# A gated cross-attention block on one core: the step of the feed-forward integers taken from the row's magnitude alone, and the last two turns in a new order

## Chip, cores and metric

The kernel runs on one core of a Trainium2 chip. Its time is the device time of one execution in microseconds (us). The engines are PE (TensorE, matrix products), PEld (its weight loads), DVE (VectorE), ACT (ScalarE), POOL (GpSimd) and SP (SyncE, which here issues DMAs). Each engine works through its own list of instructions in order; semaphores hold an instruction until what it needs is there.

## What is computed

`x` has 4 x 512 rows of 512 numbers, `ctx` 4 x 1024. An attention part with 16 heads comes first, over all 2048 rows against all 4096 context rows, with quantised queries, keys, values and weights of attention. Then comes the feed-forward part, the only one that matters here:

```python
def rms_norm(x):
    return x * jax.lax.rsqrt(jnp.mean(x * x, axis=-1, keepdims=True) + EPS)

def act_quant(x):
    scale = 127.0 / jnp.clip(jnp.max(jnp.abs(x), axis=-1, keepdims=True), 1e-05)
    q = jnp.clip(jnp.round(x * scale), -128.0, 127.0) / scale
    return x + jax.lax.stop_gradient(q - x)

def bitlinear158(x, w, b):
    xq = act_quant(rms_norm(x))
    wq = weight_quant(w)          # -1, 0 or 1, times one step for the matrix
    return jnp.einsum('bsd,od->bso', xq, wq) + b

h = jax.nn.silu(bitlinear158(x, w1, b1))      # 2048 wide
h = jax.nn.gelu(h, approximate=False)
h = layer_norm(h, ln_g, ln_b)
return bitlinear158(h, w2, b2)

x = x + jnp.tanh(g_xattn[0]) * xattn(_layernorm(x), ctx, ...)
x = x + jnp.tanh(g_ffn[0]) * ffn(_layernorm(x), ...)
```

The integers of a row are the row, divided by its largest magnitude and multiplied by 127, rounded. The factor of `rms_norm` is one number for a row, so it multiplies the row and its largest magnitude alike and falls out of the integers; it is still needed for the step by which the product of the integers is multiplied in the end.

## The kernel before

The 2048 rows are 16 tiles of 128. The attention part (about the first 1480 us) runs head by head, with an order of work that is planned by units. The feed-forward part takes the tiles in eight groups of two (`GT = 2`, `NGT = 8`). For group g, with tiles 2g and 2g + 1, these steps follow each other:

- `load_x`, `load_o`, `bias_x` (POOL adds a bias to `X`), `steps_x`, `wide_step` (ACT, L974), `turned_steps` (PE, four transposes, L987), `scale_o` (DVE, L996), `project` (PE, L1003), `residual_x` (DVE, L1009 to L1014: `X` and its mean and variance). This ends the attention part.
- `factors_x` (POOL, L892 to L900): from the variance the factor of the layer norm and of `rms_norm`, with powers. `integers_x` (DVE, L1021 to L1042): subtract the mean and multiply by the factor, largest magnitude, scale, integers. It also makes `dq1`, the step of the first product, and its inverse in three bf16 parts (L1035, L1037; on POOL for g > 0), with which the bias rides along in the product. `turned_x` (PE, L1049), `turned_x_out` (ACT, L1056).
- `hidden`: `first_product` in two halves a tile (PE, L1073, L1077; ten matmuls a half, into two PSUM buffers `ph` in turn), `silu` (ACT, L1083, scaled by `dq1`). `gelu` (ACT, L1094, with the row sum; POOL makes minus the mean of it, `nm`, at L1098). `variance` (ACT, squares of `h + nm`, L1102 by way of `squares`). `factors_h` (POOL, L907, L908): the factor `rh` of the layer norm.
- `normal` (DVE): `centred` (L1117), `normal_rows` (L1124), `magnitudes` (L1130, largest magnitude `ah`). `norm_squares` (ACT, L1102: the sum of squares `ss`). `factors_q` (POOL, L916 to L928, nine instructions): the factor of `rms_norm`, the scale `sc` of the integers and the step `dq2`.
- `integers_h` (ACT, L1181, then a transposing DMA issued by SP, L1184), `result` (PE, L1194, L1197), `bias_y` (POOL, L979), `residual_y` (DVE, L1203, then the store by SP, L1206).

`turn(s)` writes out the order for all engines of one turn by hand. It works on five groups at once: projection of group gx = s + 2, integers_x of gi = s + 1, first product, silu, gelu and variance of s, normal and norm_squares of gn = s - 1, integers_h and result of gy = s - 2. `turn` runs for s = 1 to 6; `last_turns` writes out what is left: all of group 7 (tiles t0, t1), normal and what follows of group 6 (u0, u1), and integers and results of group 5 (v0, v1). There the roots are taken by ACT (`root`, Sqrt) and some squares by DVE (`squares_dve`, L1138). On POOL a turn's list is: the three parts of integers_x's inverse, bias_x, nm of the first tile, nm of the second tile, factors_h, factors_x, factors_q, bias_y of gi.

Of the kernel before, what the change touches and what calls it, by code (L numbers as in the profile page):

```python
# [23 lines left out]
P = 128  # L24
# [9 lines left out]
def flamingo_kernel(  # L34
# [96 lines left out]
    iws = keep.tile([P, 2], F32, name="iws")  # L131

# [749 lines left out]
    def part_of(name, g, bufs=2):  # L882
        if (name, g) not in ff:
            ff[name, g] = small(name, bufs=bufs)
        return ff[name, g]

    def factors_x(g):

        v = small("vx", 2 * GT)
        a, b = v[:, :GT], v[:, GT:]  # L890
        var = ff["mv", g][:, :, 1]
        nc.gpsimd.tensor_scalar(a, var, 1.0, EPS, ALU.mult, ALU.add)  # L892

        nc.gpsimd.tensor_scalar(b, var, 1.0 + EPS, EPS * EPS, ALU.mult, ALU.add)
# [37 lines left out]

    def quant_scales(tag, a, r2, w, dq):


        nc.vector.tensor_tensor(a, a, r2, ALU.mult)
        nc.vector.tensor_scalar(a, a, 1e-5, None, ALU.max)
        sc = small(f"sc{tag}")
        nc.vector.reciprocal(sc, a)
        nc.vector.scalar_tensor_tensor(sc, sc, 127.0, r2, ALU.mult, ALU.mult)  # L940
        nc.vector.tensor_scalar(dq, a, 1.0 / 127.0, ws[:, w : w + 1], ALU.mult, ALU.mult)
        return sc
# [73 lines left out]
    def integers_x(g):  # L1016
        mv = ff.pop(("mv", g))
        r, r2 = ff.pop(("rx", g))
# [7 lines left out]
        nc.vector.tensor_reduce(a, xn, AX.X, ALU.max, apply_absolute_value=True)  # L1026
        dq = dq1[:, g * GT : (g + 1) * GT]
        sc = quant_scales("x", a, r2, 0, dq)
        xi = xis[g % 2]
        u = small("u")  # L1030
        nc.vector.reciprocal(u, dq)
        eng = nc.gpsimd if g > 0 else nc.vector
# [5 lines left out]
        for i in range(GT):  # L1038
            nc.vector.tensor_scalar(
                xn[:, i, :], xn[:, i, :], sc[:, i : i + 1], MAGIC, ALU.mult, ALU.add  # L1040
            )
            nc.vector.tensor_scalar(xi[:, i, :C], xn[:, i, :], MAGIC, None, ALU.subtract)  # L1042
# [103 lines left out]
    def root(t, name, src):  # L1146

        g, i = divmod(t, GT)
        nc.scalar.activation(
            part_of(name, g)[:, i : i + 1], ff[src, g][:, i : i + 1], AF.Sqrt,  # L1150
            bias=eps, scale=1.0 / INNER,
        )

    def inverse_h(t):
        g, i = divmod(t, GT)
        nc.vector.reciprocal(part_of("rh", g)[:, i : i + 1], ff["vh", g][:, i : i + 1])

    def scale_q(t):

        g, i = divmod(t, GT)  # L1160
        a, sd, sc, r = (
            part_of(name, g)[:, i : i + 1] for name in ("ah", "vq_", "sc", "rq")
        )
        nc.vector.tensor_scalar(a, sd, 1e-5, a, ALU.mult, ALU.max)
        nc.vector.reciprocal(sc, a)
        nc.vector.tensor_scalar(sc, sc, 127.0, None, ALU.mult)
        nc.gpsimd.tensor_tensor(r, sd, ones_n[:, :1], ALU.pow)
        dq2 = part_of("dq2", g, 3)[:, i : i + 1]
        nc.gpsimd.tensor_scalar(
            dq2, a, 1.0 / (127.0 * INT_STEP), ws[:, 1:2], ALU.mult, ALU.mult  # L1170
        )
        nc.gpsimd.tensor_scalar(dq2, dq2, r, tg2, ALU.mult, ALU.mult)

    def integers_h(t, parts=1):
# [3 lines left out]
        h = ff.pop(("h", t))  # L1178
# [40 lines left out]
    def turn(s):  # L1219
        gx, gi, gn, gy = s + 2, s + 1, s - 1, s - 2  # L1220
        last = s == NGT - 2
# [12 lines left out]
        run(integers_x, gi)  # L1234
        run(lambda t: hidden(t, 1), s, 0)
# [22 lines left out]
        run(normal, gn, 1)  # L1258
        run(gelu, s, 1)
# [7 lines left out]
        if last:  # L1267
            factors_q1(gn * GT)
# [5 lines left out]
        if last:  # L1274
            factors_q1(gn * GT + 1)
        else:
            run(factors_q, gn)
        run(bias_y, gi)

    def factors_q1(t):  # L1280

        g, i = divmod(t, GT)
        cols = columns(i)
        v, r, sc, a = (
            part_of(name, g, bufs)[:, cols]
            for name, bufs in (("vq_", 2), ("rq", 2), ("sc", 2), ("ah", 2))
        )
        nc.gpsimd.tensor_scalar(v, ff["ss", g][:, cols], 1.0 / INNER, EPS, ALU.mult, ALU.add)
        nc.gpsimd.tensor_tensor(r, v, halves[:, cols], ALU.pow)
        nc.gpsimd.tensor_scalar(a, a, r, 1e-5, ALU.mult, ALU.max)  # L1290
        nc.gpsimd.tensor_tensor(sc, a, ones_n[:, cols], ALU.pow)
        nc.gpsimd.tensor_scalar(sc, sc, r, 127.0, ALU.mult, ALU.mult)
        dq2 = part_of("dq2", g, 3)[:, cols]
        nc.gpsimd.tensor_scalar(dq2, a, 1.0 / 127.0, ws[:, 1:2], ALU.mult, ALU.mult)
        nc.gpsimd.tensor_scalar(dq2, dq2, tg2, 1.0 / INT_STEP, ALU.mult, ALU.mult)

    def last_turns():


        g = NGT - 1  # L1300
        t0, t1 = tiles(g)
        u0, u1 = tiles(g - 1)
        v0, v1 = tiles(g - 2)
        fm["junk_v"] = fm["xn"].rearrange("p a b -> p (a b)").bitcast(BF16)
        residual_y(v0 - 1)
        hidden(t0, 0)
        hidden(t0, 1)
        normal(u0)
        squares_dve(u0)
        integers_h(v0)  # L1310
        first_product(t1, 0)
        first_product(t1, 1)
        silu(t1, 0)
        silu(t1, 1)
        result(v0)
        normal(u1)
        squares_dve(u1)
        gelu(t0, True)
        gelu(t1, True)
        variance(t0)  # L1320
        root(t0, "vh", "var")
        root(u0, "vq_", "ss")
        integers_h(v1)
        centred(t0)
        inverse_h(t0)
        scale_q(u0)
        normal_rows(t0)
        magnitudes(t0)
        result(v1)
        integers_h(u0)  # L1330
        variance(t1)
        root(t1, "vh", "var")
        root(u1, "vq_", "ss")
        norm_squares(t0)
        root(t0, "vq_", "ss")
        residual_y(v0)
        centred(t1)
        inverse_h(t1)
        scale_q(u1)
        normal_rows(t1)  # L1340
        scale_q(t0)
        integers_h(u1)
        norm_squares(t1)
        root(t1, "vq_", "ss")
        magnitudes(t1)
        result(u0, fm["py"])
        integers_h(t0)
        result(u1, fm["tr"])
        scale_q(t1)
        integers_h(t1, 2)  # L1350
        for t in (v1, u0, u1):
            residual_y(t)
        for t in (t0, t1):
            result(t)
        for t in (t0, t1):
            residual_y(t)

    def at_unit(i, n, *fs_):
        plan[i, n].extend(fs_)
# [29 lines left out]
    at_unit(TWO + 7, 1, partial(vector_for_ffn, "b2", tg2))  # L1389
    at_unit(201, 0, take_values)  # L1390
# [23 lines left out]
    with tc.manual_schedule():  # L1414
# [127 lines left out]
        for s in range(1, NGT - 1):  # L1542
            turn(s)
# [33 lines left out]
```

## Time and profile before

| What | Value |
|---|---|
| Median of three runs | 1753.49 us (1747.51 to 1753.80) |
| Span of the profiled execution | 1752.0 us |
| Busy: DVE, PE, ACT, POOL, PEld | 1603.4, 1362.5, 1346.7, 1276.9, 588.5 us |
| Turn 2 on PE (from its first transposes to those of turn 3) | 1562.57 to 1591.33 us |
| Turns 3 and 4 on PE | 1591.33 to 1617.91, 1617.91 to 1644.49 us |
| First product of group 6 begins (PE) | 1671.30 us |
| First product of group 7 begins (PE) | 1693.07 us |
| Last result on PE begins, last residual_y | 1744.08, 1748.14 us |

Times in the text are microseconds from the start of the profiled execution. A row of the timeline gives start, length, engine, line of the kernel, operation, what it writes and reads, and in brackets the idle time of that engine just before and who ended it. The names of buffers are those of the memory in which they lie, which the feed-forward part takes over from the attention part: `kT`, `skb`, `pT`, `s`, `vq`, `rT` there are rows, integers and results of the feed-forward part.

### The profile page before, as it was taken

The page shows a single profiled execution, that of the slowest core. Times are in us where ns is not written, and L with a number is a line of the kernel's source. Part 1 is how long each engine was busy: PE and PEld are TensorE (multiplying, and loading weights), DVE is VectorE, ACT ScalarE, POOL GpSimd, SP SyncE. Part 2 cuts the span into 40 slices and gives each one's busy share as a digit, 9 for nine tenths or more (in the row PEclk, how much of TensorE's full clock was granted, in tenths as well). Part 3 has the DMA queues.
Part 4 walks back from the last instruction along what each step waited for, and adds up shares of the span by engine and source line. Part 5 has one row for each costly group of instructions (what it writes and reads, how often), then busy time and mean ns, then how long its engine had stood idle before and what let it go on. Part 6 is the DMA issues. An engine that isn't in the chain of part 4 may idle for free. (4 is left out here: it accounts for less than half of the span.)

```text
span 1752.0 us, 31542 instructions
## 1 busy us (share of the span) xinstructions
PE 1362.5 (78%) x12164; PEld 588.5 (34%) x12174; DVE 1603.4 (92%) x2232; ACT 1346.7 (77%) x994; POOL 1276.9 (73%) x1276
## 2 busy tenths in 40 slices
PE   8999967788875888885587888646666577789985
PEld 4444422333322333332233333222222233334432
DVE  5786899999999999999999999999999989489995
ACT  2443467988887788888788888878887877679986
POOL 0001226999997889998899999879999998456763
PEclk9999975655555555555556555555555555889998
DMA  6876869999988999998999999889999866713324
GB/s 204 277 246 228 284 190 217 212 197 213 187 182 177 211 191 217 210 176 186 169 218 191 211 207 192 180 164 205 161 181 173 174 115 125 184 32 84 85 60 96
DMA packets 736264, 315.93 MB, mean 180 GB/s; under 512 B 657993, under 2 KB 703593, under 8 KB 729714
## 3 DMA queue, kind: packets, MB, share of 16 engines
q1 hardware_dynamic: 727058, 308.66, 81.1%
q10 hardware_dynamic: 9024, 5.24, 1.1%
q8 instruction: 95, 1.56, 0.4%
q14 instruction: 55, 0.45, 0.1%
q0 software_dynamic: 32, 0.01, 0.0%
HBM read 110.15 MB, written 40.12 MB: 86 GB/s over the span
## 5 line engine op out<-in xcount | busy, mean ns | idle before, releaser
L743 POOL CAST rT<-pT 128x2048 int16<-128x2048 uint8 x506 | 945.0, 1894 | 27.9 <-issue 6.8
L689 DVE CUSTOM_DVE_ANT_0 s<-ps_s,skb 128x1536 f32<-128x1536 f32 x531 | 808.4, 1574 | 24.5 <-PE ps_s L680 15.9
L709 ACT ACTIVATE r<-s,nb,sq 128x4096 uint8<-128x4096 f32 x177 | 673.0, 3803 | 145.6 <-POOL nb L706 110.1
L680 PE MATMUL ps_s<-kT,qT 32*128 32x512 bf16 x2048 | 456.6, 586 | 297.2 <-DVE m L689 285.3
L689 DVE CUSTOM_DVE_ANT_0 third<-ps_s,skb 128x1536 f32<-128x1536 f32 (+1 forms) x237 | 361.9, 1574 | 4.0 <-PE ps_s L680 2.4
L709 ACT ACTIVATE r<-third,nb,sq 128x4096 uint8<-128x4096 f32 x79 | 300.5, 3803 | 56.9 <-POOL nb L706 26.4
L680 PEld LDWEIGHTS <-qT 32*128 32x128 bf16 x2048 | 96.8, 99 | 622.1 <-issue 613.7
L759 PE MATMUL acc<-rT,vq 128*32 128x128 f16 x8192 | 262.6, 305 | 26.0 <-ACT o L770 17.6
L759 PEld LDWEIGHTS <-vq 128*32 128x32 f16 x8192 | 194.9, 136 | 138.3 <-issue 104.7
L613 PE MATMUL vacc<-fx 128*128 128x256 f32 x384 | 228.1, 696 | 0.0
L704 POOL TENSOR_SCALAR m<-m 128x1 f32<-128x1 f32 x256 | 93.1, 364 | 97.5 <-DVE m L689 92.3
L451 POOL TENSOR_SCALAR nsq<-sq 128x16 f32<-128x16 f32 x16 | 3.3, 205 | 174.6 <-DVE sq L282 174.6
L613 PEld LDWEIGHTS vacc<-fx 128*128 128x128 f32 x384 | 93.5, 302 | 81.9 <-issue 81.5
L414 PE MATMUL kacc<-wk_sb,cT 128*128 128x512 f32 x256 | 116.8, 599 | 0.0
L706 POOL TENSOR_SCALAR nb<-m,nsq 128x1 f32<-128x1 f32 x256 | 67.3, 263 | 25.1
L1073 PE MATMUL ph<-fx,skb 128*128 128x512 bf16 x246 | 70.3, 409 | 3.4 <-ACT s L1083 2.3
L689 DVE DVE_READ_ACCUMULATOR2_ANT m<- 128x1 f32 x768 | 62.7, 82 | 0.0
L414 PEld LDWEIGHTS kacc<-wk_sb,cT 128*128 128x128 f32 x256 | 46.8, 193 | 46.9 <-issue 45.9
L414 PE MATMUL qacc<-wq_sb,xT 128*128 128x512 f32 x128 | 57.7, 593 | 0.2 <-ACT xT L291 0.2
L436 DVE TENSOR_TENSOR f<-kacc,bk_sb 128x512 f32<-128x512 f32 x32 | 22.0, 689 | 34.4 <-PE kacc L414 33.3
L291 ACT COPY cT<-tr 128x512 f32<-128x512 f32 x32 | 18.6, 580 | 33.6 <-PE tr L290 33.4
L1083 ACT ACTIVATE s<-ph,dq 128x1024 f32<-128x1024 f32 x24 | 26.6, 1113 | 23.1 <-PE ph L1077 23.1
(244 smaller groups left out, 1406.6 us busy)
## 6 DMA issues: line engine op xcount, KB each, us to landing
skb<-skd SPq DMA_DIRECT2D x32, 1024.0 KB
fx<-cTd SPq DMA_DIRECT2D x48, 512.0 KB
wt<-in_L_ffn_w_dram SPq DMA_DIRECT2D x16, 1024.0 KB
in<-in_ctx_dram SPq DMA_DIRECT2D x32, 256.0 KB
cTd<-cT SPq DMA_DIRECT2D x8, 1024.0 KB
q4d<-rows4q SPq DMA_DIRECT2D x16, 512.0 KB
vtd<-fx SPq DMA_DIRECT2D x24, 256.0 KB
fx<-vtd SPq DMA_DIRECT2D x24, 256.0 KB
```

Source lines behind the costliest of these rows:

```text
L414: nc.tensor.matmul(acc, tT[:, c, :], wk_sb[c] if kind == "k" else wq_sb[:, c, :], start=(c == 0), stop=(c == CC - 1),)
L436: nc.vector.tensor_tensor(f, acc, bk_sb, ALU.add)
L613: nc.tensor.matmul(state["acc"], wv_g[:, c, :], state["cT", j][:, c, :], start=(c == 0), stop=(c == CC - 1),)
L680: nc.tensor.matmul(ps_s[:, b * KB - k0 : (b + 1) * KB - k0], qT[rows, 0, t * P : (t + 1) * P], kT[rows, 0, a * KB : (a + 1) * KB], start=True,
L689: nc.vector.tensor_tensor_reduce(s[:, k0 : k0 + w], ps_s[:, :w], skb[:, k0 : k0 + w], 1.0, -3.0e38, ALU.mult, ALU.max, m3[:, n : n + 1],)
L704: nc.gpsimd.tensor_scalar(m, m3[:, 0:1], m3[:, 1:2], m3[:, 2:3], ALU.max, ALU.max)
L706: nc.gpsimd.tensor_scalar(nb, m, nsq[:, t, h : h + 1], LN255, ALU.mult, ALU.add)
L709: nc.scalar.activation(r.rearrange("p (n two) -> p two n", two=2), s.rearrange("p (two n) -> p two n", two=2), AF.Exp, bias=nb, scale=sq[: ...
L743: cast(spreads[k][:, 2 * u : 2 * u + 2, :, :] .bitcast(I16) .rearrange("p a (two b) q -> p a two (b q)", two=2), pTs[u][:, :, k * NW : (k ...
L759: nc.tensor.matmul(acc[c * HD : (c + 1) * HD, :], vq[:, kb, h % HPG * HD : (h % HPG + 1) * HD], rT[:, c, b, :], start=(k == 0 and b == 0), ...
L1073: nc.tensor.matmul(ph[:, n, :], xqT[:, c, tok], w1T[:, c, at : at + 512], start=(c == 0), stop=False,)
L1083: nc.scalar.activation(ff["h", t][:, n2 * 1024 : (n2 + 1) * 1024], ph.rearrange("p n w -> p (n w)"), AF.Silu, scale=dq1[:, t : t + 1],)
```

## The change

The scale of the integers is taken from the largest magnitude alone, without the factor of `rms_norm`; the factor goes into the steps `dq1` and `dq2` only. So the scale can be made before the squares, and the roots can come after the integers.

- `factors_x` makes one product more and multiplies by the weight's step (two POOL instructions more).
- `integers_x` subtracts the mean only, takes the scale from the magnitude (a tensor_scalar and a reciprocal on DVE), makes the integers at once, and then `dq1` and its inverse, for g > 0 on POOL (a product and a power there in place of DVE instructions).
- A new `steps_h` makes the scale `sc` from `ah`: on POOL with a power in `turn`, on DVE with a reciprocal in `last_turns`. In `turn` it stands behind `normal` of the second tile of gn and ahead of `gelu` of the second tile of s.
- `factors_q` keeps four of its nine instructions. A new constant `wst` holds the product that two of the old ones multiplied in.
- `bias_y` of a group moves from the end of one turn to behind `integers_x` in the next.
- `turn` runs for s = 1 to 5; `last_turns` writes out the order of the rest anew, without Sqrt on ACT. `root`, `inverse_h`, `scale_q`, `factors_q1` and `quant_scales` go. Small tiles of `part_of` get three buffers in place of two.

```diff
@@ factors_x
         nc.gpsimd.tensor_tensor(r2, r2, y[:, GT:], ALU.mult)
-        ff["rx", g] = y[:, :GT], r2
+        nc.gpsimd.tensor_tensor(r2, r2, y[:, :GT], ALU.mult)
+        nc.gpsimd.tensor_scalar(r2, r2, ws[:, 0:1], 1.0, ALU.mult, ALU.mult)
+        ff["rx", g] = r2
...
+    def steps_h(g, i=None, eng=None):
+        cols = columns(i)
+        a, sc = part_of("ah", g)[:, cols], part_of("sc", g)[:, cols]
+        if eng is None:
+            nc.gpsimd.tensor_scalar(a, a, EPS**1.5, 1.0 / 127.0, ALU.max, ALU.mult)
+            nc.gpsimd.tensor_tensor(sc, a, ones_n[:, cols], ALU.pow)
+        else:
+            eng.tensor_scalar(a, a, EPS**1.5, 1.0 / 127.0, ALU.max, ALU.mult)
+            eng.reciprocal(sc, a)
@@ factors_q
         nc.gpsimd.tensor_tensor(r, v, halves[:, cols], ALU.pow)
-        a = ff["ah", g][:, cols]
-        nc.gpsimd.tensor_tensor(a, a, r, ALU.mult)
-        nc.gpsimd.tensor_scalar(a, a, 1e-5, 1.0, ALU.max, ALU.mult)
-        sc = part_of("sc", g)[:, cols]
-        nc.gpsimd.tensor_tensor(sc, a, ones_n[:, cols], ALU.pow)
-        nc.gpsimd.tensor_scalar(sc, sc, 127.0, 0.0, ALU.mult, ALU.add)
-        nc.gpsimd.tensor_tensor(sc, sc, r, ALU.mult)
         dq2 = part_of("dq2", g, 3)[:, cols]
-        nc.gpsimd.tensor_scalar(dq2, a, 1.0 / 127.0, ws[:, 1:2], ALU.mult, ALU.mult)
-        nc.gpsimd.tensor_scalar(dq2, dq2, tg2, 1.0 / INT_STEP, ALU.mult, ALU.mult)
+        nc.gpsimd.tensor_tensor(dq2, ff["ah", g][:, cols], r, ALU.mult)
+        nc.gpsimd.tensor_scalar(dq2, dq2, wst, 1.0, ALU.mult, ALU.mult)
@@ integers_x
-            nc.vector.tensor_scalar(
-                xn[:, i, :], X[t], mv[:, i, 0:1], r[:, i : i + 1],
-                ALU.subtract, ALU.mult,
-            )
+            nc.vector.tensor_scalar(xn[:, i, :], X[t], mv[:, i, 0:1], None, ALU.subtract)
         a = small("ax")
         nc.vector.tensor_reduce(a, xn, AX.X, ALU.max, apply_absolute_value=True)
+        nc.vector.tensor_scalar(a, a, EPS * EPS, 1.0 / 127.0, ALU.max, ALU.mult)
+        sc = small("scx")
+        nc.vector.reciprocal(sc, a)
+        xi = xis[g % 2]
+        for i in range(GT):
...
+        eng = nc.gpsimd if g > 0 else nc.vector
         dq = dq1[:, g * GT : (g + 1) * GT]
-        sc = quant_scales("x", a, r2, 0, dq)
...
+        eng.tensor_tensor(dq, a, ff.pop(("rx", g)), ALU.mult)
         u = small("u")
-        nc.vector.reciprocal(u, dq)
+        if g > 0:
+            nc.gpsimd.tensor_tensor(u, dq, ones_n[:, :GT], ALU.pow)
+        else:
+            nc.vector.reciprocal(u, dq)
@@ turn
         run(integers_x, gi)
+        if s > 1:
+            run(bias_y, s)
...
         run(normal, gn, 1)
+        run(steps_h, gn)
         run(gelu, s, 1)
...
-        run(bias_y, gi)
+        run(factors_q, gn)
@@ last_turns (the new order from the first product of group 6; w0, w1 are group 4)
+        residual_y(w0 - 1); hidden(u0, 0); integers_x(g); hidden(u0, 1)
+        integers_h(w0); hidden(u1, 0); integers_h(w1); normal(v0); scale(v0)
+        hidden(u1, 1); turned_x(t0); gelu(u0); result(w0); turned_x_out(t0)
+        turned_x(t1); normal(v1); scale(v1); bias_y(g - 1); gelu(u1)
+        variance(u0); factors_h(g - 1, 0); turned_x_out(t1); result(w1)
+        residual_y(w0); integers_h(v0); centred(u0); residual_y(w1)
+        hidden(t0, 0); hidden(t0, 1); normal_rows(u0); variance(u1)
+        factors_h(g - 1, 1); centred(u1); magnitudes(u0); scale(u0)
+        first_product(t1, 0); result(v0); first_product(t1, 1); silu(t1, 0)
+        integers_h(v1); silu(t1, 1); normal_rows(u1); gelu(t0, True)
+        variance(t0); factors_h(g, 0); gelu(t1, True); centred(t0)
+        magnitudes(u1); scale(u1); result(v1); variance(t1); factors_h(g, 1)
+        integers_h(u0); bias_y(g); normal_rows(t0); centred(t1)
+        magnitudes(t0); scale(t0); integers_h(u1); norm_squares(v0)
+        factors(v0); result(u0, fm["py"]); residual_y(v0); integers_h(t0)
+        normal_rows(t1); magnitudes(t1); scale(t1); norm_squares(v1)
+        factors(v1); result(u1, fm["tr"]); integers_h(t1, 2)
+        norm_squares(u0); factors(u0); norm_squares(u1); factors(u1)
+        residual_y(v1); squares_dve(t0); factors(t0); result(t0)
+        squares_dve(t1); factors(t1); result(t1)
+        for t in (u0, u1, t0, t1):
+            residual_y(t)
```

In the last part of the diff the calls stand several to a line; `scale(t)` is `steps_h` on DVE for one tile, `factors(t)` is `factors_q` for one tile.

More of the change, by code (lines that the diff above doesn't have):

```diff
@@ L131, in flamingo_kernel @@
     iws = keep.tile([P, 2], F32, name="iws")
+    wst = keep.tile([P, 1], F32, name="wst")
     def stats_of(pool, t, n):
@@ L880, in columns, with part_of @@
         return slice(0, GT) if i is None else slice(i, i + 1)
-    def part_of(name, g, bufs=2):
+    def part_of(name, g, bufs=3):
         if (name, g) not in ff:
@@ L918, in factors_q @@
         nc.gpsimd.tensor_tensor(r, v, halves[:, cols], ALU.pow)
-        a = ff["ah", g][:, cols]
-        nc.gpsimd.tensor_tensor(a, a, r, ALU.mult)
-        nc.gpsimd.tensor_scalar(a, a, 1e-5, 1.0, ALU.max, ALU.mult)
-        sc = part_of("sc", g)[:, cols]
-        nc.gpsimd.tensor_tensor(sc, a, ones_n[:, cols], ALU.pow)
-        nc.gpsimd.tensor_scalar(sc, sc, 127.0, 0.0, ALU.mult, ALU.add)
-        nc.gpsimd.tensor_tensor(sc, sc, r, ALU.mult)
         dq2 = part_of("dq2", g, 3)[:, cols]
-        nc.gpsimd.tensor_scalar(dq2, a, 1.0 / 127.0, ws[:, 1:2], ALU.mult, ALU.mult)
-        nc.gpsimd.tensor_scalar(dq2, dq2, tg2, 1.0 / INT_STEP, ALU.mult, ALU.mult)
+        nc.gpsimd.tensor_tensor(dq2, ff["ah", g][:, cols], r, ALU.mult)
+        nc.gpsimd.tensor_scalar(dq2, dq2, wst, 1.0, ALU.mult, ALU.mult)
     def has(g):
         return 0 <= g < NGT
[L933 to L942, printed above, removed]
     ff = {}
@@ L1017, in integers_x @@
         mv = ff.pop(("mv", g))
-        r, r2 = ff.pop(("rx", g))
         xn = fm["xn"]
         for i, t in enumerate(tiles(g)):
-            nc.vector.tensor_scalar(
-                xn[:, i, :], X[t], mv[:, i, 0:1], r[:, i : i + 1],
-                ALU.subtract, ALU.mult,
-            )
+            nc.vector.tensor_scalar(xn[:, i, :], X[t], mv[:, i, 0:1], None, ALU.subtract)
         a = small("ax")
         nc.vector.tensor_reduce(a, xn, AX.X, ALU.max, apply_absolute_value=True)
+        nc.vector.tensor_scalar(a, a, EPS * EPS, 1.0 / 127.0, ALU.max, ALU.mult)
[3 more added lines that the diff above has]
+        for i in range(GT):
+            nc.vector.tensor_scalar(
+                xn[:, i, :], xn[:, i, :], sc[:, i : i + 1], MAGIC, ALU.mult, ALU.add
+            )
+            nc.vector.tensor_scalar(xi[:, i, :C], xn[:, i, :], MAGIC, None, ALU.subtract)
+        eng = nc.gpsimd if g > 0 else nc.vector
         dq = dq1[:, g * GT : (g + 1) * GT]
-        sc = quant_scales("x", a, r2, 0, dq)
-        xi = xis[g % 2]
+        eng.tensor_tensor(dq, a, ff.pop(("rx", g)), ALU.mult)
         u = small("u")
-        nc.vector.reciprocal(u, dq)
-        eng = nc.gpsimd if g > 0 else nc.vector
+        if g > 0:
+            nc.gpsimd.tensor_tensor(u, dq, ones_n[:, :GT], ALU.pow)
+        else:
+            nc.vector.reciprocal(u, dq)
         for n in range(3):
@@ L1037, in integers_x @@
                 eng.tensor_tensor(u, u, part[:, :, 0], ALU.subtract)
[L1038 to L1042, printed above, removed]
     def turned_x(t):
@@ L1144, in norm_squares @@
         squares(t, part_of("ss", g)[:, i : i + 1])
[L1146 to L1172, printed above, removed]
     def integers_h(t, parts=1):
@@ L1177, in integers_h @@
         hT = fm["hT"].next()
-        h = ff.pop(("h", t))
+        h = ff["h", t]
         for n in range(parts):
@@ L1220, in turn @@
         gx, gi, gn, gy = s + 2, s + 1, s - 1, s - 2
-        last = s == NGT - 2
         def run(f, g, *i):
@@ L1266, in turn @@
         run(norm_squares, gn, 0)
-        if last:
-            factors_q1(gn * GT)
         run(result, gy, 1)
@@ L1273, in turn, with scale, factors @@
         run(norm_squares, gn, 1)
[L1274 to L1277, printed above, removed]
-        run(bias_y, gi)
[L1280 to L1295, printed above, removed]
+        run(factors_q, gn)
     def last_turns():
+        def scale(t):
+            steps_h(t // GT, t % GT, nc.vector)
+        def factors(t):
+            factors_q(t // GT, t % GT)
         g = NGT - 1
@@ L1303, in last_turns @@
         v0, v1 = tiles(g - 2)
-        fm["junk_v"] = fm["xn"].rearrange("p a b -> p (a b)").bitcast(BF16)
-        residual_y(v0 - 1)
+        w0, w1 = tiles(g - 3)
+        residual_y(w0 - 1)
+        hidden(u0, 0)
+        integers_x(g)
+        hidden(u0, 1)
+        integers_h(w0)
+        hidden(u1, 0)
+        integers_h(w1)
+        normal(v0)
+        scale(v0)
+        hidden(u1, 1)
+        turned_x(t0)
+        gelu(u0)
+        result(w0)
+        turned_x_out(t0)
+        turned_x(t1)
@@ L1306, in last_turns @@
+        normal(v1)
+        scale(v1)
+        bias_y(g - 1)
+        gelu(u1)
+        variance(u0)
+        factors_h(g - 1, 0)
+        turned_x_out(t1)
+        result(w1)
+        residual_y(w0)
+        integers_h(v0)
+        centred(u0)
+        residual_y(w1)
         hidden(t0, 0)
         hidden(t0, 1)
-        normal(u0)
-        squares_dve(u0)
-        integers_h(v0)
+        normal_rows(u0)
+        variance(u1)
+        factors_h(g - 1, 1)
+        centred(u1)
+        magnitudes(u0)
@@ L1311, in last_turns @@
+        scale(u0)
         first_product(t1, 0)
+        result(v0)
         first_product(t1, 1)
         silu(t1, 0)
+        integers_h(v1)
         silu(t1, 1)
-        result(v0)
-        normal(u1)
-        squares_dve(u1)
+        fm["junk_v"] = fm["xn"].rearrange("p a b -> p (a b)").bitcast(BF16)
+        normal_rows(u1)
         gelu(t0, True)
+        variance(t0)
+        factors_h(g, 0)
         gelu(t1, True)
-        variance(t0)
-        root(t0, "vh", "var")
-        root(u0, "vq_", "ss")
@@ L1323, in last_turns @@
-        integers_h(v1)
         centred(t0)
-        inverse_h(t0)
-        scale_q(u0)
+        magnitudes(u1)
+        scale(u1)
+        result(v1)
+        variance(t1)
+        factors_h(g, 1)
+        integers_h(u0)
+        bias_y(g)
         normal_rows(t0)
+        centred(t1)
         magnitudes(t0)
[L1329 to L1335, printed above, removed]
+        scale(t0)
@@ L1336, in last_turns @@
+        integers_h(u1)
+        norm_squares(v0)
+        factors(v0)
+        result(u0, fm["py"])
         residual_y(v0)
-        centred(t1)
-        inverse_h(t1)
-        scale_q(u1)
+        integers_h(t0)
         normal_rows(t1)
[L1341 to L1344, printed above, removed]
         magnitudes(t1)
-        result(u0, fm["py"])
-        integers_h(t0)
+        scale(t1)
+        norm_squares(v1)
+        factors(v1)
         result(u1, fm["tr"])
-        scale_q(t1)
@@ L1350, in last_turns @@
         integers_h(t1, 2)
[L1351 to L1355, printed above, removed]
+        norm_squares(u0)
+        factors(u0)
+        norm_squares(u1)
+        factors(u1)
+        residual_y(v1)
+        squares_dve(t0)
+        factors(t0)
+        result(t0)
+        squares_dve(t1)
+        factors(t1)
+        result(t1)
+        for t in (u0, u1, t0, t1):
             residual_y(t)
@@ L1389, in flamingo_kernel @@
     at_unit(TWO + 7, 1, partial(vector_for_ffn, "b2", tg2))
+    at_unit(
+        TWO + 7, 1,
+        partial(
+            nc.gpsimd.tensor_scalar, wst, ws[:, 1:2], tg2, 1.0 / INT_STEP, ALU.mult, ALU.mult
+        ),
+    )
     at_unit(201, 0, take_values)
@@ L1541, in flamingo_kernel @@
             wide_step(t)
-        for s in range(1, NGT - 1):
+        for s in range(1, NGT - 2):
             turn(s)
```

## The prediction

> **What bounds the kernel now.** I read the page first (DVE 92%, POOL 73%, PE 78%), then the stages, then the chain that ended last, then the timeline of single turns. All that the change touches, but for one product on POOL and the first two groups' integers, lies after 1535 us. The stages, 30 us each (columns: stretch, length, busy time of PE, PEld, DVE, ACT, POOL, clock, DMA share, GB/s):
>
> ```profile
> 1610.00:1640.00 30.00, 29.95 (x121) 12.56 (x122) 29.31 (x33) 28.14 (x28) 18.64 (x28) 1.00 0.36 88
> 1640.00:1670.00 30.00, 29.95 (x122) 12.21 (x122) 28.99 (x33) 28.20 (x30) 18.17 (x29) 1.00 0.24 53
> 1700.00:1730.00 30.00, 15.53 (x46) 4.79 (x46) 25.73 (x22) 25.00 (x27) 18.29 (x18) 0.67 0.32 61
> ```
>
> In the steady turns PE never idles, DVE and ACT hardly do, POOL has 11 us of 30 free. In the last stage no engine is full. The chain says the same: it stays on PE through turns 2 to 5, then leaves it.
>
> ```profile
> 1614.21 3.45 PE acc L1194 x16
> 1617.98 0.59 PE tr L987 x4
> 1618.62 0.81 PE ph L1073 x3
> ...
> 1721.17 5.32 DMA rT<-vq
> 1726.53 5.68 PE acc L1194 x16
> ```
>
> A turn is 1591.33 to 1617.91 on PE, 26.6 us; DVE's own turn is 26.2 (1589.53 to 1615.71). So less work on DVE alone buys nothing there, and a wait of PE costs its full length. The rows of turn 2 that decide the forecast (start, length, engine, line, operation; the bracket is idle time and who ended it):
>
> ```profile
> 1583.98 3.65 PE L1003 MATMUL py<-third,vq 128*128 128x512 f32 x8
> ...
> 1584.99 2.00 ACT L1102 ACTIVATE kT<-pT,nm 128x2048 uint8<-128x2048 f32 x1 [0.20 <-POOL nm L1098]
> ...
> 1587.16 0.19 POOL L907 TENSOR_SCALAR vh<-var 128x2 f32<-128x2 f32 x1 [2.21 <-ACT kT L1102]
> 1587.33 2.29 DVE L1130 TENSOR_REDUCE ah<-s 128x1 f32<-128x2048 f32 x1
> 1587.44 0.72 POOL L908 TENSOR_TENSOR rh<-vh,halves 128x2 f32<-128x2 f32 x1
> ...
> 1589.46 0.60 ACT L974 COPY kT<-step 128x512 f32<-128x512 f32 x1
> 1589.53 0.74 DVE L1009 SCALAR_TENSOR_TENSOR rT<-py,tg,rT 128x512 f32<-128x512 f32 x1
> ...
> 1591.33 0.66 PE L987 MATMUL tr<-ident,kT 128*128 128x128 f32 x4
> ...
> 1592.43 0.68 DVE L996 TENSOR_TENSOR qT<-tr,qT 128x512 f32<-128x512 f32 x1
> ```
>
> The variance of tile 5 (L1102, ACT) starts at 1584.99, as soon as POOL has written its nm. The magnitudes of the group before (L1130, DVE) end only at 1589.5. Between the two is the whole forecast.
>
> **Steps_h, the costly edit.** It stands on POOL between nm of a turn's first tile and nm of its second, and needs both magnitudes of group gn. POOL runs its list in order, so the second nm, until now free to go at 1584.9, stands behind the reduction that ends at 1589.5. Steps_h is a tensor_scalar and a pow: 0.28 and 0.72 as L907 and L908; nm 0.27, hops 0.08. So nm is there at 1589.5 + 1.35 = 1590.85 and the variance is 5.9 us late. Behind steps_h on POOL stand that nm, then factors_h and factors_x; queued behind the variance on ACT: the copy L1056, the squares of the group before, both wide_steps, the table load and the next silu. PE's transposes L987 wait for the first wide_step: it ended at 1590.06, now 1595.95, and they start at 1596.05 in place of 1591.33: PE idles 4.7 us. Scale_o follows them 0.7 later, 1596.8 for 1592.43, so DVE, which had no idle time there, is 4.4 us late, and on DVE lie the next integers_x, both normals and again the reduction for which steps_h waits. That is a closed loop: each turn pays.
>
> Per turn: 26.2 of DVE + 4.4 - 0.6 (saved in integers_x, below) = 30.0; against what these three turns take at L1130 (1589.5 to 1668.4, 26.3 each) 3.7 more. Turn 1 has the larger gap: its variance started at 1557.43, the reduction ends at 1563.5, so 7.4 late; the transposes go from 1562.57 to 1570.0, scale_o from 1565.07 to 1570.7, 5.6, less 0.6: 5.0. Turns 2 to 4: 3 x 3.7 = 11.1. In turn 5 the variance is 4.5 late (1665.26 against 1668.43 + 1.35); no transposes follow, but the first silu of group 6 goes from 1673.75 to 1678.2, its second, once 2.6 behind it, comes 1.0 behind: 2.9 late enters the end.
>
> **The clock after a gap.** A gap of 2.83 us on PE was followed by half speed (four matmuls in 1.89, then 1.04):
>
> ```profile
> 1562.57 0.66 PE L987 MATMUL tr<-ident,kT 128*128 128x128 f32 x4 [2.83 <-ACT kT L974]
> ...
> 1565.04 1.89 PE L1073 MATMUL ph<-fx,skb 128*128 128x512 bf16 x4
> 1566.86 0.39 PE L1077 MATMUL ph<-third,skb 9*128 9x512 bf16 x1
> 1567.17 1.04 PE L1073 MATMUL ph<-fx,skb 128*128 128x512 bf16 x4
> ```
>
> It lasted some 4 us and cost 2. A gap of 2.99 at 1681.8 was followed by full speed, so the price lies between 0 and 2 a gap. The new gaps are longer than either; I take 2 less the 0.6 that DVE gains ahead of the second transposes: 1.4, for turns 2 to 5, 5.6. [...]
>
> **Integers_x.** Small DVE work from L936 to the first L1039 (1595.38 to 1596.40, 1.02) becomes a tensor_scalar and a reciprocal (0.21 and 0.20 start to start): 0.6 less. DVE no longer waits for yx; that wait was 1.05 once and 1.72 in the lead-in, hidden by PE's order both times. POOL takes on two operations in factors_x (0.6) and a product and pow (1.1), and loses five of factors_q's nine, 2.2 of the 4.1 us between 1593.70 and 1597.83; with steps_h 0.6 more of POOL a turn, covered by its 11 free; without that cover 0.6 x 5 = 3. dq1 now comes from POOL some 3 us later; the silu that reads it is 20 us on. For group 0, nine small DVE operations, several held behind POOL's casts (1.82, 1.61, 1.78), become seven behind the same casts: between -2 and +1, taken as 0.
>
> **Bias_y** goes from behind factors_q to behind integers_x's part on POOL. It lay over L1117 and L1124 (2.76 and 3.24 for 2.33 and 2.35: 1.3 us of DVE) and still does: 0, between -1.3 and +1.3 a turn. bias_x is behind it and residual_x waits for that; it ends about as before, no margin. wst is one small operation, 0.3 at most.
>
> **The end.** From the first product of group 6 to the last store: 1671.30 to 1752.0, 80.7 us. Out go the sqrt table load (1.28), six roots of 0.2, and two squares of ACT before the last integers (4.0, now on DVE behind them). I walked the new list from that first product. PE: four half-products 10.3, results of 8 and 9 with their waits 11.7, t's first product at 22.0 (old 21.8); two halves, one half, result, half: 14.2; silu, load, gelu, nm, variance 6.6: 42.8. Then DVE, in its order: centred, magnitudes, scale, normal_rows, centred, magnitudes, scale, residual_y, normal_rows, magnitudes, scale: seven of 2.2 to 2.4, three of 0.4, one of 0.7, and 1.8 behind bias_y and factors: 62.5. Integers of t1 2.4, transposes 3.4, result 3.9: 72. POOL's last factors come out at 75 (four in a row after ACT's last squares, 1.5 to 1.8 each), residual and store 4: 79. On SP the stores of w0, w1 and v0 now stand ahead of transposes; by the walk each residual_y is done before the integers that follow, v0's by 1 us only. So -1.6; as the walk of the old list also came out 1.1 short, I take 0, between -10 (below) and +4. [...]
>
> **Sum.** 5.0 + 11.1 + 2.9 + 5.6 + 0 = 24.6, and 0.6 for a short PE gap behind the late silu: 25.2. On the profiled 1752.0 that is 1777; the median of the runs is 1.5 above it: 1779.
>
> **Rivals.** (a) It does not bite: ACT's late variance falls into slack. For it: ACT idles 1.46 before its second silu and 0.2 to 0.7 before its first, each turn. Against: 5.9 is needed, and wide_step was only 1.3 ahead of the transposes. Then PE sets the turns as before, and with the end at 0 it is 1752.0 + 1.5: 1753, 7%. (b) The other side: no bite, and the end gains in full. ACT's last integers come earlier by all that leaves ACT, 6.5, and v1's result (PE idle 14.1 before 1726.53) no longer queues ahead of them: 3 to 4 more, -10, 1743. It decides only if DVE's row above is not the chain, and nm is on time: 5%. (c) It bites harder: bias_x, last in POOL's late queue and without margin, holds residual_x too, 3 us in each of four turns: 1791, 10%. The forecast: 78%.
>
> **Range.** Warm gaps and a gain of 4 at the end give 1769, cold ones and a loss of 5 1785. To leave out no more than 2 in 10 it runs from 1765 to 1791. This measurement tells about 0.5% (8.8 us; the three runs span 6) from no change: faster 5%, same 7%, slower 88%.
>
> **What would show it.** In turns 2 to 4 PE idles 4 to 5 us before L987's first transposes, ended by wide_step; ACT idles over 5 us before its second variance, ended by POOL's nm; POOL waits for DVE's ah. The turn on PE is 30 to 32. From the first product of group 6 the end takes 80 to 86. Wrong if nm of the second tile still follows its gelu within a microsecond, or if the end is shorter by more than 5.

## The result, and the profile after

The changed kernel takes 1782.93 us (median of four runs, 1774.9 to 1789.82); the kernel before, run beside it, 1753.64 (1747.51 to 1755.8, four runs). The ratio is 1.0173, with a 95% interval of 1.0154 to 1.0192: slower, by 29.3 us where the forecast had 25.2. The profiled execution spans 1783.4 us, 31.4 more than the one before.

The new line numbers, for the rows below: L970 wide_step, L983 turned_steps, L992 scale_o, L999 project, L1071 and L1075 first_product, L1081 silu, L1092 gelu, L1096 nm, L1100 squares (variance and norm_squares), L1115, L1122 and L1128 normal, L920 and L921 steps_h on POOL, L923 and L924 steps_h on DVE, L935 the last of factors_q, L1151 integers_h, L1164 and L1167 result, L1173 residual_y.

The stages first (stretch, length, busy time of PE, PEld, DVE, ACT and POOL, clock, DMA share, GB/s). The first two are turns, the last is in the end.

```profile
1600.00:1630.00 30.00, 28.39 (x99) 11.02 (x101) 22.51 (x23) 21.06 (x21) 11.38 (x23) 0.83 0.29 68
1630.00:1660.00 30.00, 26.27 (x87) 9.65 (x86) 18.34 (x23) 22.86 (x23) 12.57 (x27) 0.77 0.41 89
1740.00:1770.00 30.00, 16.28 (x62) 6.07 (x63) 24.03 (x20) 22.43 (x21) 12.48 (x14) 0.77 0.40 79
```

DVE, which had 29 busy us in 30 in the steady turns, has 22.5 and 18.3, and no other engine is full either. PE's 28 and 26 are not more work: the clock that was 1.00 is 0.83 and 0.77. With room on every engine, these stretches must be bound by a chain that goes round several of them. The chain of waits shows it whole (start, length, engine, what it writes, line):

```profile
1592.64 2.30 DVE ah L1128
...
1595.01 0.25 POOL ah L920
...
1595.33 0.72 POOL sc L921
1596.04 0.18 POOL nm L1096
...
1598.83 2.00 ACT kT L1100 x2
1600.83 0.52 ACT kT L970
1601.39 1.11 PE tr L983 x4
```

This is the loop that was forecast, in its order: DVE's magnitudes, the scale on POOL, behind it the mean nm of the second tile, ACT's variance and what stands behind it, wide_step, PE's transposes. From there the chain goes over PE and DVE to the next L1128 at 1626.94 and round again. The same moments in the timeline, with the idle time in brackets:

```profile
1595.01 0.24 POOL L920 TENSOR_SCALAR ah<-ah 128x2 f32<-128x2 f32 x1 [7.76 <-DVE ah L1128]
...
1596.25 2.00 ACT L1100 ACTIVATE kT<-pT,nm 128x2048 uint8<-128x2048 f32 x1 [4.82 <-POOL nm L1096]
...
1601.39 1.11 PE L983 MATMUL tr<-ident,kT 128*128 128x128 f32 x4 [3.97 <-ACT kT L970]
...
1602.60 0.69 DVE L992 TENSOR_TENSOR qT<-tr,qT 128x512 f32<-128x512 f32 x1 [4.39 <-PE tr L983]
```

One wait of 7.8 us on POOL, which is no bottleneck, comes back as 4.8 on ACT, 4.0 on PE and 4.4 on DVE. But a turn on PE is longer than that: turns 2 to 5 are 32.43, 34.29, 35.80 and 28.40 us (before 28.76, 26.58, 26.58, 26.81; a turn is counted from its first transposes, turn 5 to the first product of group 6). Four rows of PE in turn 4 tell why (the columns as above):

```profile
1635.68 1.11 PE L983 MATMUL tr<-ident,kT 128*128 128x128 f32 x4 [3.51 <-ACT kT L970]
...
1641.32 1.89 PE L1071 MATMUL ph<-fx,skb 128*128 128x512 bf16 x4
...
1646.03 1.11 PE L983 MATMUL tr<-ident,skb 128*128 128x128 f32 x4
...
1648.71 1.04 PE L1071 MATMUL ph<-fx,skb 128*128 128x512 bf16 x4
```

Four transposes take 1.11 in place of 0.66, four products 1.89 in place of 1.04, and not for some 4 us as in the rows of before, but for 12.3: until 1647.94. Short stretches show where the clock changes (columns as in the stages; five in turn 3, two in turn 4):

```profile
1596.75:1600.16 3.41, 0.67 (x3) 0.09 (x1) 1.16 (x2) 3.41 (x4) 1.42 (x5) 1.00 0.56 187
1600.16:1603.57 3.41, 1.97 (x6) 1.30 (x8) 0.97 (x2) 3.41 (x6) 1.71 (x5) 0.50 0.83 275
1603.57:1606.99 3.42, 3.42 (x8) 0.63 (x6) 3.25 (x8) 1.47 (x3) 2.71 (x7) 0.50 0.00 0
1606.99:1610.40 3.41, 3.41 (x9) 0.96 (x9) 0.55 (x2) 1.11 (x1) 3.12 (x7) 0.50 0.00 0
1610.40:1613.81 3.41, 3.41 (x17) 1.27 (x14) 1.97 (x2) 2.56 (x2) 2.90 (x3) 1.00 0.02 5
...
1630.88:1634.29 3.41, 1.29 (x6) 0.34 (x4) 1.33 (x2) 3.41 (x4) 1.27 (x4) 1.00 0.56 166
1634.29:1647.94 13.65, 12.04 (x30) 4.29 (x32) 5.53 (x12) 7.96 (x10) 10.59 (x20) 0.50 0.24 76
```

In all nine traces the clock takes two values, 1.00 and 0.50, and changes only on a grid: every stretch between two changes is a whole number of steps of 3.41 us. In turns 2 to 5 half speed lasts 10.24, 10.24, 13.65 and 3.41 us, which is three, three, four steps and one; counted from when PE works again, 3.9, 9.0, 12.3 and 3.4. In turn 2 the clock fell at 1562.61, 6.4 us before PE had anything to do, so most of its half speed passed in the gap.

The end, from the first product of group 6 (1699.88) to the last store, takes 83.5 us for 80.7 before.

### The profile page after: what moved, and what is told of

Same layout as the page of the kernel before. It is cut to its first block, busy times and chain, and to the rows that moved or that the text cites. A ratio compares the mean times of both kernels' runs of the same rounds, so it can differ in the third digit from the quotient of the medians.

```text
span 1783.4 us, 31518 instructions
## 1 busy us (share of the span) xinstructions
PE 1363.3 (76%) x12163; PEld 590.8 (33%) x12174; DVE 1599.2 (90%) x2200; ACT 1344.6 (75%) x987; POOL 1268.2 (71%) x1296
## 3 DMA queue, kind: packets, MB, share of 16 engines
q10 hardware_dynamic: 9024, 5.24, 1.1%
## 5 line engine op out<-in xcount | busy, mean ns | idle before, releaser
L681 PE MATMUL ps_s<-kT,qT 32*128 32x512 bf16 x2048 | 451.6, 579 | 311.1 <-DVE m L690 298.2
L614 PE MATMUL vacc<-fx 128*128 128x256 f32 x384 | 224.0, 685 | 0.0
L1071 PE MATMUL ph<-fx,skb 128*128 128x512 bf16 x245 | 75.3, 433 | 4.2 <-ACT s L1081 2.5
L1081 ACT ACTIVATE s<-ph,dq 128x1024 f32<-128x1024 f32 x24 | 26.6, 1112 | 31.7 <-PE ph L1075 31.6
L458 ACT COPY rows4q<-rows4q 128x1536 bf16<-128x1536 bf16 x16 | 23.5, 1471 | 27.0 <-DVE rows4q L143 26.9
```

The costliest lines, as they stand in the source:

```text
L458: nc.scalar.copy(r4[:, :, 1:, :], r4[:, :, 0:1, :].to_broadcast([P, H, HPG - 1, HD]))
L614: nc.tensor.matmul(state["acc"], wv_g[:, c, :], state["cT", j][:, c, :], start=(c == 0), stop=(c == CC - 1),)
L681: nc.tensor.matmul(ps_s[:, b * KB - k0 : (b + 1) * KB - k0], qT[rows, 0, t * P : (t + 1) * P], kT[rows, 0, a * KB : (a + 1) * KB], start=True,
L1071: nc.tensor.matmul(ph[:, n, :], xqT[:, c, tok], w1T[:, c, at : at + 512], start=(c == 0), stop=False,)
L1081: nc.scalar.activation(ff["h", t][:, n2 * 1024 : (n2 + 1) * 1024], ph.rearrange("p n w -> p (n w)"), AF.Silu, scale=dq1[:, t : t + 1],)
```

## The experiments

Two batches, each beside runs of the kernel before on the same chip. In the first that kernel took 1752.42 us (19 runs), in the second 1753.24 (11 runs).

**Where the scale stands.** Is it the place of steps_h on POOL, and that alone? The first kernel is the changed one with the call moved past both means:

```diff
         run(normal, gn, 1)
-        run(steps_h, gn)
         run(gelu, s, 1)
         run(variance, s, 0)
         run(variance, s, 1)
         factors_h(s)
+        run(steps_h, gn)
```

> The changed kernel with one call moved: in turn, steps_h stands behind factors_h, so nm of the second tile is free again. Theory of the wait: the turns go back to 26 to 27 us on PE, ACT's second variance follows its gelu at once, and the whole is 1750 to 1757, about the kernel before. Rival, the other edits (POOL's new work in integers_x, the moved bias_y, the new end) cost a good part: it stays above 1765.

Measured: 1751.89 us, ratio 0.9994 [0.9979, 1.0008]. All of the loss is gone. PE's first transposes of turn 3, and what went before them on POOL and ACT in turn 2:

```profile
1592.30 0.66 PE L983 MATMUL tr<-ident,kT 128*128 128x128 f32 x4
```

```profile
1584.48 1.28 POOL L1096 TENSOR_SCALAR nm<-sg 128x1 f32<-128x1 f32 x1 [1.35 <-ACT pT L1092]
...
1586.48 2.00 ACT L1100 ACTIVATE kT<-pT,nm 128x2048 uint8<-128x2048 f32 x1
...
1590.51 0.24 POOL L920 TENSOR_SCALAR ah<-ah 128x2 f32<-128x2 f32 x1 [0.86 <-DVE ah L1128]
```

No bracket on PE: it never idles there. nm waits for its own gelu, the second variance follows the first at once, and steps_h waits for the magnitudes at a place where nobody is behind it in a hurry. Turns 3 and 4 are 26.58 us, as before the change. The end of this kernel is 77.4 us (first product of group 6 at 1672.04, span 1749.4): the new order of the last part gains 3.3 when nothing enters it late.

**The wait without the rest of the change.** The opposite: the kernel before, with nothing but two POOL instructions in steps_h's place, whose result nobody uses.

```diff
+    def wait_alone(g):
+        w = small("wt_")
+        nc.gpsimd.tensor_scalar(w, ff["ah", g], 1.0, 0.0, ALU.mult, ALU.add)
+        nc.gpsimd.tensor_tensor(w, w, ones_n[:, :GT], ALU.pow)
...
         run(normal, gn, 1)
+        if s < 6:
+            run(wait_alone, gn)
         run(gelu, s, 1)
```

> The kernel before with the wait alone: in turns 1 to 5 two small POOL instructions that read both magnitudes of gn stand ahead of nm of the second tile; their result is not used. Theory of the wait: PE idles some 10 us ahead of turn 2 and 3 to 5 ahead of turns 3 to 5, and the time is 1774 to 1790, as much as the whole change cost. Rival, the change's other edits carry the loss: 1753 to 1762.

Measured: 1787.03 us, ratio 1.0199 [1.0177, 1.0222]. Less than 1 us of POOL work a turn costs 35.

```profile
1592.35 0.19 POOL L1221 TENSOR_SCALAR wt__17990<-ah 128x2 f32<-128x2 f32 x1 [7.31 <-DVE ah L1130]
1592.63 0.72 POOL L1222 TENSOR_TENSOR wt__17990<-wt__17990,ones_n 128x2 f32<-128x2 f32 x1
1593.33 0.19 POOL L1098 TENSOR_SCALAR nm<-sg 128x1 f32<-128x1 f32 x1
```

The three rows are the mechanism: the two instructions are short, but nm stands behind them in one list, and they stand behind DVE. The old end, entered late in the same way, takes 85.2 us here (1696.94 to 1782.1) against 80.7: coming in late costs the end 4.5.

**The same scale on another engine.** If POOL's list is the point, the scale may stay where it is in the program when DVE makes it, behind its own reduction:

```diff
-        run(steps_h, gn)
+        run(lambda g: steps_h(g, None, nc.vector), gn)
```

> The changed kernel with steps_h of the turns on DVE (tensor_scalar and reciprocal, 0.2 us each) in the same place. POOL's list holds nothing ahead of the second nm. Theory of the wait: 1750 to 1757, within 2 of the version with the call moved, since DVE gives back the 0.4 a turn that integers_x saved, under PE's turn. Rival, any work added at this place costs: above 1762.

Measured: 1750.22 us, ratio 0.9987 [0.9975, 0.9999]. Turns 3 and 4 are 26.58, and the end is 77.2. DVE's two instructions, 0.17 each, cost PE nothing.

**The clock, apart from the gap.** Here the changed kernel keeps its wait, and PE gets throwaway products in front of the transposes, so that it waits at work:

```diff
+    def fill(n):
+        ph = fm["ph"].views[fm["ph"].n % 2]
+        for _ in range(n):
+            nc.tensor.matmul(ph[:, 0, :], ident_b, w1T[:, 0, :512], start=True, stop=True)
...
         run(residual_y, gy - 1, 1)
+        if s > 1:
+            fill(40 if s == 2 else 16)
         run(turned_steps, gx, 0)
```

> The changed kernel with matmuls of no use in PE's gaps: 40 of 512 columns ahead of turn 2 and 16 ahead of turns 3 to 5, results overwritten; the wait is untouched. If the clock's part of the loss is what the profile of after shows (half speed for 4, 9, 12 and 4 us, some 12 us lost in all, of which DVE's slack hides a few), PE keeps full clock there and the time falls by 6 to 11, to 1772 to 1777; the turns then take 30 to 31. Rival, the loop alone makes the long turns and the clock hides behind DVE: within 2 of 1783.

Measured: 1773.87 us (1773.05 to 1776.81, four runs), ratio 1.013 [1.0106, 1.0153].

```profile
1628.09 3.63 PE L1192 MATMUL ph<-fx,ident_b 128*128 128x512 bf16 x16
1632.55 0.66 PE L983 MATMUL tr<-ident,kT 128*128 128x128 f32 x4 [0.83 <-ACT kT L970]
1633.04 1.03 PE L1071 MATMUL ph<-fx,skb 128*128 128x512 bf16 x4
```

ACT's waits for nm are as long as ever (5.24, 5.24 and 5.07 us in turns 3 to 5), the transposes are as late, but at full speed, and all three turns take 31.05, 31.04 and 31.05 us. So the loop by itself is 31.05 us, and what the changed kernel has above it, 1.4, 3.2 and 4.8 us in turns 2 to 4, is the clock. By the medians the clock costs 9.1 us (1782.93 less 1773.87), by the difference of the two ratios 7.5. More work on PE made the kernel faster.

**How long a gap.** The last question on the clock: need the gap be filled, or only shortened? 34 products in turn 2 leave 2.95 us of its long gap idle; 6 in turns 3 to 5 take 1.2 us off each.

```diff
-            fill(40 if s == 2 else 16)
+            fill(34 if s == 2 else 6)
```

> The changed kernel with 34 throwaway products ahead of the first transposes of turn 2 and 6 ahead of those of turns 3 to 5 (filled_gaps had 40 and 16): some 1.3 us of each gap is filled, the rest stays idle, about 2.5 to 3 us. If the clock falls only after a gap longer than about 3 us, the transposes stay at full speed (0.66 for four) and a turn takes 31.05 us as in filled_gaps: 1772 to 1776. If 2.8 us is enough (as turn 2 of before showed once, while 2.99 once was not), the transposes run at 1.1 and the turns take 32 to 36: 1779 to 1787.

Measured: 1774.39 us (1770.15 to 1779.78, four runs), ratio 1.0127 [1.0108, 1.0146].

```profile
1570.66 0.66 PE L983 MATMUL tr<-ident,kT 128*128 128x128 f32 x4 [2.95 <-ACT kT L970]
1571.15 1.81 PE L1071 MATMUL ph<-fx,skb 128*128 128x512 bf16 x4
...
1602.94 0.66 PE L983 MATMUL tr<-ident,kT 128*128 128x128 f32 x4 [2.63 <-ACT kT L970]
1603.43 1.03 PE L1071 MATMUL ph<-fx,skb 128*128 128x512 bf16 x4
...
1633.98 0.66 PE L983 MATMUL tr<-ident,kT 128*128 128x128 f32 x4 [2.99 <-ACT kT L970]
1634.47 1.03 PE L1071 MATMUL ph<-fx,skb 128*128 128x512 bf16 x4
```

Gaps of 2.63 and 2.99 us leave the clock alone, and turns 3 and 4 take 31.04 again; 3.51 had halved it for 12.3 us. Turn 2 is the exception: after its 2.95 us the transposes still run at full speed and the products behind them at half, for 3.41 us, and it takes 32.28. The same happens in the kernel before and in every kernel here that has a gap of 2.8 to 2.95 at that place. So a gap's length doesn't decide alone. The steps of the clock's grid tell the two apart (turn 2, then turn 3; the first number behind the length is PE's work):

```profile
1567.85:1571.26 3.41, 0.60 (x5) 0.58 (x6) 0.00 (x0) 3.41 (x6) 2.76 (x9) 1.00 0.00 0
1571.26:1574.67 3.41, 3.41 (x9) 0.83 (x7) 3.12 (x7) 3.05 (x3) 1.51 (x5) 0.50 0.00 0
...
1598.57:1601.98 3.41, 1.57 (x7) 0.53 (x7) 0.90 (x2) 3.41 (x4) 1.69 (x5) 1.00 0.67 215
1601.98:1605.39 3.41, 2.45 (x13) 1.18 (x13) 1.67 (x4) 3.39 (x7) 1.44 (x6) 1.00 0.79 245
```

Turn 2's gap lies nearly whole in one step, and at the end of that step, 0.6 us after the gap, the clock falls. A point of the grid divides the gap of turn 3, neither step loses 2 us of work, and the clock stays. In the nine traces all 114 steps at full speed with at least 2 us of idle PE are followed by half speed, and none with less than 1 us; between these it goes both ways (1.83 in the step from 1682.93 on kept the clock in the kernel before, 1.40 lost it at 1679.53 in scale_on_dve), so idle time in a step is not the whole rule.

**A better end.** The mechanism asks for one thing: let no instruction that is needed soon stand behind one that waits long. In scale_on_dve's end DVE idles 5.5 us for a variance, POOL 9.5, and PE 12.2 for integers of group 6 whose scale was made long before. The next kernel is scale_on_dve with its last part in this order (from behind the first silu of t1, several calls to a line):

```diff
         integers_h(v1)
+        norm_squares(v0); factors(v0)
         silu(t1, 1)
...
         normal_rows(u1)
+        magnitudes(u1); scale(u1); bias_y(g)
         gelu(t0, True); variance(t0); factors_h(g, 0)
+        integers_h(u0)
         gelu(t1, True); centred(t0)
-        magnitudes(u1); scale(u1)
-        result(v1); variance(t1); factors_h(g, 1)
-        integers_h(u0); bias_y(g)
-        normal_rows(t0); centred(t1); magnitudes(t0); scale(t0)
+        result(v1); residual_y(v0); variance(t1); factors_h(g, 1)
+        normal_rows(t0); magnitudes(t0); scale(t0)
         integers_h(u1)
-        norm_squares(v0); factors(v0)
         result(u0, fm["py"])
-        residual_y(v0)
         integers_h(t0)
+        centred(t1)
         normal_rows(t1); magnitudes(t1); scale(t1)
         norm_squares(v1); factors(v1)
         result(u1, fm["tr"])
-        integers_h(t1, 2)
         norm_squares(u0); factors(u0)
+        integers_h(t1, 2)
```

> The kernel of scale_on_dve with its last part in another order: the second magnitudes of group 6 fill DVE's idle 5.5 us ahead of centred(t0); DVE then normalises t0 and takes its magnitudes before it starts on t1; ACT makes the first integers of group 6 between the variance of t0 and the gelu of t1, and two of the four squares earlier; bias_y of group 7 moves up to a stretch in which POOL idles 9.7 us. Theory (in the end DVE's order and ACT's integers set the time, and POOL's last four factors behind ACT's late squares hold the last residuals): t1's integers come 3.4 us earlier, the last residual_y 4 to 5, so the end from group 6's first product is 72 to 74 us in place of scale_on_dve's, and the time 1743 to 1748. Rival (DMA or PE's four results in a row set the end): less than 1.5 us is gained, 1749 to 1752.

Measured: 1746.18 us, ratio 0.9962 [0.9948, 0.9975]; the end is 72.1 us (1670.28 to 1742.4), 5.1 shorter than scale_on_dve's. The ratio is 0.0025 below scale_on_dve's, some 4 us, and the two intervals meet at 0.9975. From the two timelines, scale_on_dve first, then this kernel, PE's first result of group 6 and ACT's last integers:

```profile
1721.16 4.96 PE L1164 MATMUL py<-pT 128*128 128x512 f16 x16 [12.17 <-DMA pT<-r]
```

```profile
1719.63 5.43 PE L1164 MATMUL py<-pT 128*128 128x512 f16 x16 [7.78 <-DMA pT<-r]
...
1728.90 2.37 ACT L1151 ACTIVATE vq<-s,c,sc 128x1024 int16<-128x1024 f32 x2 [1.39 <-DVE sc L924]
```

Counted from the first product of group 6, the result starts 49.4 us later in place of 54.0 (1721.16 less 1667.20), the last integers 58.6 in place of 62.2 (1729.42 in scale_on_dve), and the last residual_y 68.2 in place of 73.4 (1738.49 and 1740.55): the order of the lists set the end, not the transfers or PE's four results.

**And turn 2's gap.** The gap of 2.8 us before turn 2's transposes, which was there before the change, can be filled too:

```diff
+        if s == 2:
+            fill(12)
         run(turned_steps, gx, 0)
```

> end_tightened with 12 throwaway products (128x512) on PE ahead of turn 2's first transposes, where before and scale_on_dve idle 2.8 us and then run at half speed. Theory (a gap that is filled keeps the clock, and the half speed there costs what that turn is longer than the others, 28.2 against 26.6 us): turn 2 takes 26.6 to 27 us, the time is 1 to 1.6 us below end_tightened's. Rival (DVE's own 26 us a turn, with PE's first rows waiting for the same wide_step, sets turn 2): same time as end_tightened within 0.5 us.

Measured: 1743.54 us, ratio 0.9953 [0.9941, 0.9966]: faster than both kernels of this study, by 0.5% and 2.2%. Turn 2 takes 26.59 us (1564.47 to 1591.06) for 28.17 in end_tightened, as the theory had it, and the clock is full from 1545.63 to 1712.89, where end_tightened has 3.41 us of half speed from 1562.89 on. That the whole time follows is likely but not shown: the intervals of the two overlap, and the medians differ by 2.6.

## Why the prediction was right, and where it was off

**Steps_h, the costly edit: right.** Behind the next four calls it costs nothing, put alone into the old kernel it costs 35 us. What would show it was named and is there: POOL waits for ah, nm is late, PE idles 4.0, 3.5 and 3.5 before the transposes of turns 3 to 5, ended by wide_step, DVE 4.4 behind that. ACT idles 7.55 once, then 4.82 and 4.36 for the more than 5 forecast: in filled_gaps, where PE is at full speed, the same waits are 5.1 to 5.3. The turns of 30 to 32 on PE are not there: they are 32.4, 34.3 and 35.8, and 31.05 without the clock's part.

**The clock after a gap: right in kind, too small, and the step that failed.** "I take 2 less the 0.6": 1.4 a gap, 5.6 in all, from one place in which half speed had lasted some 4 us (one step of the grid, 1563.46 to 1566.87). Measured are 7.5 to 9.1 by the runs and 11.4 by the two profiles (31.4 less the 20.0 of filled_gaps): 1.4, 3.2 and 4.8 us in turns 2 to 4, 1.8 in turn 5 (28.40 against 26.58) and 1.7 in the end (83.5 against 81.8; whether that is the clock was not tried) are 12.9, less 1.5 by which the first transposes of turn 2 came earlier in this execution than in that of filled_gaps. One short gap, behind which half speed had lasted one step, gave its length for longer gaps, behind which it lasted up to four. Half of 9.0 and 12.3 us is 4.5 and 6.1, of which 3.2 and 4.8 reached the turn, above the bound of 2 that I had put.

What the traces show of the fall and of the way back: before the transposes of turns 3 and 4, gaps of 2.63 and 2.99 us kept the clock (gaps_partly_filled), and gaps of 3.48 (turn 3 of wait_alone) to 10.29 us (turn 2 of the changed kernel) lost it. Those of 2.83 to 2.95 before turn 2 lost it too: in the kernel before, PE idled for 2.57 of the 3.41 us from 1560.05 on, and at the end of that step the clock fell. The step from 1603.57 to 1606.99 of the changed kernel, full of work, did not bring it back. So neither the gap's length alone nor one step of work is enough to reckon with.

**The loop: 30.0 forecast, 31.05 measured.** "26.2 of DVE + 4.4 - 0.6" is missing 1.05. The timeline of filled_gaps gives the pieces: L1115 of the first tile takes 3.33 in place of 2.76 (with L1122's 3.18 for 3.24 that is +0.5 in the term of bias_y, 0 between -1.3 and +1.3; bias_y lies over all of L1115 in both kernels, and why it costs more now was not tried), and DVE idles 0.56 before the second scale_o, where integers_x had become 0.6 shorter: PE's second transposes come last there. So the saving in integers_x was worth nothing.

```profile
1607.83 0.69 DVE L992 TENSOR_TENSOR qT<-tr,qT 128x512 f32<-128x512 f32 x1 [0.56 <-PE tr L983]
1608.44 3.33 DVE L1115 SCALAR_TENSOR_TENSOR pT<-pT,nm,skb 128x2048 f32<-128x2048 f32 x1
```

**The end: 0 forecast, -3.3 measured, and a late entry of 4.5 for 2.9 + 0.6.** In the sum these two misses and the loop's nearly cancel, by luck: without the clock the forecast was 19.6, and filled_gaps' profile has 20.0 more than before's. The last residuals do come late for the reason given, POOL's factors behind ACT's last squares:

```profile
1774.83 0.75 DVE L1173 SCALAR_TENSOR_TENSOR r<-py,dq,r 128x512 f32<-128x512 f32 x1 [1.35 <-POOL dq L935]
1776.37 0.75 DVE L1173 SCALAR_TENSOR_TENSOR r<-tr,dq,r 128x512 f32<-128x512 f32 x1 [0.79 <-POOL dq L935]
```

**Integers_x of group 0: 0, as taken.** From the first of its DVE rows to the last it takes 13.8 us before and 14.3 in scale_behind: the integers that came earlier in the list still stood beside POOL's casts and additions (L1024 and L1027 took 1.38 to 1.99 us each there, 0.43 to 0.48 in the kernel before, where POOL idled beside them).

**The rivals.** (a) and (b), "it does not bite", fall with wait_alone. (b)'s other half, an end 10 shorter, also: it is 3.3. (c), bias_x late, is not seen: no row of DVE in turns 2 to 5 of the changed kernel waits for it.

**What stays open.** In the profiles scale_behind and scale_on_dve are 4.4 and 4.1 us shorter than the kernel before from the attention part's last row on, in the medians 0.5 and 2.2; their intervals reach to 3.7 and 4.4 us shorter. Between profiled executions that last row lies anywhere from 1477.1 to 1482.5 us, so that small differences of two spans tell nothing. And why half speed lasts one step of the clock's grid after one gap and three or four after another is not shown: the step full of work from 1563.46 on in the kernel before ended it, the one from 1603.57 on in the changed kernel did not.

## What to carry to other kernels

A short instruction that is put into an engine's list costs what stands behind it, not what it takes: ask for each such place when its operands come, and which result behind it somebody else needs before that; two POOL instructions of 0.9 us a turn cost 35 us here, and nothing four calls further down or on the engine that makes their operand. When an edit opens a gap on PE, its cost is not the gap alone: two gaps of 3.5 to 4 us cost 3.2 and 4.8 more in clock, and filling a part of each took that away. What counted was not the gap's length alone, but how much of one step of the clock's 3.41 us grid it filled: 2 us or more lost the clock in all 114 such steps of these traces. A span in which every engine has slack is read by the chain of waits, not by busy time.

## What the hardware did that I had not expected

- The clock changed only on a grid of 3.41 us, in every trace. After gaps of 3.97 and 3.51 us PE ran at half speed for 9.0 and 12.3 us of nearly unbroken work, after one of 10.29 us for only 3.9, because the first 6.4 us of its three steps had passed in the gap.
- Throwaway products in those gaps made the kernel 7.5 to 9 us faster. Its runs lay within 3.8 us of each other, those of the changed kernel within 14.9; but those of wait_alone, with its gaps unfilled, lay within 5.5 (four runs each), so that the spread is not shown to be the clock's.
- Gaps of 2.63 to 2.99 us kept the clock in turns 3 and 4; one of 2.83 to 2.95 before turn 2 lost it in five kernels, 0.6 to 0.9 us behind the gap, at the end of the step that the gap had filled.
